# Layer 2 of a two-layer graph attention network on one core: who adds x, who sums the last rows of a tile, who makes the second norm's statistics

## The chip, the cores and the metric

The kernel runs on one core of one Trainium2 chip. The metric is the device time of one execution in microseconds (us). The kernel before the change has a median of 5286.99 us in three runs (5283.68 to 5294.54). Engines are called as the profile calls them: PE is TensorE (PEld its weight loads), DVE is VectorE, ACT is ScalarE, POOL is GpSimd, SP is SyncE.

## The reference, cut to what matters

Two layers of graph attention over 10000 nodes and 170000 edges (80000 in both directions and a loop for each node), with a layer norm and a residual behind each, and one more layer norm at the end. The change touches layer 2 (one head, 768 columns) and what follows it:

```python
def gat_conv(x, edge_index, W, a_src, a_dst, bias, heads, out_ch, concat):
    ...
    alpha = e / (s[dst] + 1e-16)                       # softmax over the edges of a node
    msg = xl[src] * alpha[:, :, None]
    out = jax.ops.segment_sum(msg, dst, num_segments=n)
    ...
h = gat_conv(h, edge_index, W2, a_src2, a_dst2, b2, 1, OUT_DIM, False)
h = layer_norm(h, g2, be2)
h = h + (h1 @ Wr2 + br2)
...
x = _layernorm(x + h)                                  # the second norm: no scale, no shift
```

## The kernel before, in words

**Layers and tiles.** Nodes are sorted by their number of edges and cut into 79 tiles of 128 nodes. Every node of a tile gets the same number n of edge places, so that a tile is n "rows": row k holds, on each of the 128 partitions, the 770 numbers (768 columns and two logits) of the k-th neighbour of that partition's node. There are 1371 rows in all, some 17 a tile. The order of tiles (`turns`) mixes long and short ones; in the middle of layer 2 tiles of 15 and 20 rows alternate. Layer 1 ends about 3200 us into the span, layer 2 fills the rest.

**The ring.** Rows of layer 2 lie in a ring of `RING2` = 41 places (`ring`). POOL fetches each by an indirect DMA (line 472), in order; a tile's first row, the node's own, comes by SP instead (line 501). `ring.fetch(FIRST[t] + k + 1 + ring.size)` stands behind row k in the loop, so a place is fetched anew when both engines that use its row are done with it.

**Two engines sum a tile.** DVE adds columns 0 to 511 of each row, times the row's weight, to an accumulator in SBUF (`acc`, in `weigh`, line 573): one SCALAR_TENSOR_TENSOR a row. PE adds columns 512 to 767 (`summed` in `weights_of`): for each row ACT multiplies the identity by the weights of the 128 nodes (line 1298, the "diagonal"), and PE multiplies the diagonal with the row's 256 columns (line 1299) into PSUM, into columns 768 to 1023 of the same PSUM tile `big` that holds the tile's residual. An f32 matmul is two matmuls in the profile. Diagonals lie in 5 buffers of 4 (`DIAGONALS`, `G`): a buffer is used anew when all 4 matmuls of its last use are done.

**The residual.** `residual(t)` makes h1 @ Wr2 on PE: for 512 and then for 256 columns, first x, by a matmul with the identity (line 1350), then the 8 pieces of h1 (line 1353). x and h1 of a tile come by SP (`fetch_x`, lines 1257 and 1258), two tiles ahead.

**The norms.** `norms(t, ...)` is a generator that runs in four pieces in the loop of the next tile: (1) ahead of row 0, DVE makes the statistics of the first norm (`deviation`: BN_STATS, line 584, of two pieces of `acc` and of PE's 256 columns in `big`; BN_AGGR, line 586), ACT makes the inverse deviation by Ln and Exp (lines 588, 589); (2) at row 3, DVE scales and shifts (lines 598, 600), adds the residual (line 1363) and makes the statistics of the second norm (lines 584, 586, on `w`), ACT its inverse deviation; (3) at row 6, DVE makes minus mean over deviation (line 1367) and ACT the output (line 1369); (4) at row 9, POOL scatters it to DRAM (line 1371).

**The order.** All engines run their instructions in the order in which the program writes them. In the loop of tile t it is: `residual(t + 1)` on PE; piece 1 of `norms(t - 1)`; then the rows, and between them the other pieces, the softmax weights of tile t + 1 (`weights_of`, at row `turn`, some 5 or 6, and 3 rows later, DVE and ACT) and, with those, the diagonals and PE's matmuls for tile t + 1. Three of the 79 tiles are so long that their softmax is made in two parts (`cuts_of` gives three cuts).

Of the kernel before, what the change touches and what calls it, by code (L numbers as in the profile page):

```python
# [28 lines left out]
F32 = mybir.dt.float32  # L29
# [6 lines left out]
P = 128  # L36
# [16 lines left out]
DIAGONALS = 5  # L53
ON_PE2 = 512
SHARE = 4
# [31 lines left out]
def gnn_kernel(ctx, tc, x, x_cols, src, dst, src_col, dst_col, W1, a_src1, a_dst1, b1, g1, be1, Wr1, br1,  # L87
# [757 lines left out]
    def begin_layer2(mem):  # L845


        rest = mem.shape[1]

        def at_end(n):  # L850
            nonlocal rest
            rest -= n
            return mem[:, rest:rest + n]

        firsts = [(at_end(C1), at_end(D0)) for _ in range(min(2, NT))]
        for t, (hT, xt) in enumerate(firsts):
            nc.sync.dma_start(hT, h1_d[turns[t]])
            nc.sync.dma_start(xt, x_d[turns[t]])
# [376 lines left out]
    def ordered_layer2(mem, begun):  # L1235
# [4 lines left out]
        with tc.tile_pool(name="b2", bufs=1) as pool, tc.tile_pool(name="small2", bufs=2) as small, \  # L1240
# [4 lines left out]
            parts = pieces(w2.rearrange("p k n -> p (k n)")[:, :6 * C1], C1)  # L1245
            held = mem.shape[1] // R2
# [4 lines left out]
            def fetch_x(t):  # L1251

                if t < 2:
                    hT, xt = firsts[t]
                else:
                    hT, xt = parts[t % 2], parts[2 + t % 2][:, :D0]
                    nc.sync.dma_start(hT, h1_d[turns[t]])
                    nc.sync.dma_start(xt, x_d[turns[t]])
                return hT.rearrange("p (k n) -> p k n", n=P), xt

            ins = {0: fetch_x(0)}
# [3 lines left out]
            ins[1] = fetch_x(1)  # L1265
# [20 lines left out]
            def weights_of(t):  # L1286
# [7 lines left out]
                def summed(e, lo, hi, more=None, m=0):  # L1294
                    for k in range(lo, hi):
                        if (k - lo) % G == 0:
                            diagonals = pool.tile([P, G, P], F32, name="diagonals", bufs=DIAGONALS)
                        nc.scalar.activation(diagonals[:, (k - lo) % G, :], ident, AF.Copy, scale=e[:, k - lo, :])  # L1298
                        nc.tensor.matmul(to, diagonals[:, (k - lo) % G, :], ring.slot(at + k)[:, ON_PE2:C2],  # L1299
                                         start=False, stop=(k == n - 1), skip_group_check=True)  # L1300
                        if k - lo < m:
                            nc.tensor.matmul(more, diagonals[:, (k - lo) % G, :], ring.slot(at + k)[:, :ON_PE2],
                                             start=False, stop=(k - lo == m - 1), skip_group_check=True)
# [15 lines left out]
                summed(e, 0, cuts[1])  # L1319
# [23 lines left out]
            def residual(t):  # L1343


                hT, xt = ins.pop(t)
                r = ps_big.tile([P, 2 * BANK], F32, name="big")
                for c in range(0, C2, BANK):
                    d = min(C2, c + BANK)
                    nc.tensor.matmul(r[:, c:d], ident, xt[:, c:d], start=True, stop=False,  # L1350
                                     skip_group_check=True)
                    for j in range(K1):
                        nc.tensor.matmul(r[:, c:d], hT[:, j, :], wr2[:, j, c:d], start=False,  # L1353
                                         stop=(j == K1 - 1 and d < C2),
                                         skip_group_check=True)
                return r

            def norms(t, h, r, means):
# [8 lines left out]
                nc.vector.scalar_tensor_tensor(less, mean, -1.0, inv, op0=OP.mult, op1=OP.mult)  # L1367
                o = pool.tile([P, C2], F32, name="out")
                nc.scalar.activation(o, h, AF.Identity, bias=less, scale=inv)
# [14 lines left out]
            for t in range(NT):  # L1384
# [19 lines left out]
                for k in range(n):  # L1404
# [11 lines left out]
                    else:  # L1416
# [15 lines left out]
                if t + 2 < NT and t + 2 not in ins:  # L1432
                    ins[t + 2] = fetch_x(t + 2)
# [273 lines left out]
```

## Time and profile before

| | |
|---|---|
| time, median of 3 runs | 5286.99 us (5283.68 to 5294.54) |
| the profiled execution | 5287.85 us, span 5286.1 us, mean granted PE clock 0.943 |
| busy over the span: PE, DVE, ACT, POOL | 4742.8 (90%), 4326.7 (82%), 3084.4 (58%), 3432.3 (65%) us |
| moved over the span | HBM read 1426.26 MB, written 177.29 MB, 303 GB/s |

The profile is of one execution. Each row of a group says: line, engine, operation, output from inputs by the program's names, shapes, count; then busy us and mean ns of one; then the idle time of the engine just ahead of these instructions, and what ended most of it ("issue": nothing that the profile shows; "remote": a semaphore from elsewhere). `w` in a name is the SBUF memory of the layer's weights W2, which layer 2 uses again for h1, x and the normed tile. A row of the timeline says: start, duration, engine, line, operation, names, shape, count, and the idle time ahead of it.

### The profile page before, as it was taken

What the parts mean: (1) busy time and instruction counts of PE and PEld (TensorE: products, weight loads), DVE (VectorE), ACT (ScalarE), POOL (GpSimd) and SP (SyncE); (2) the same over time, 40 slices, a digit from 0 to 9 for tenths busy, and PEclk for the clock granted to TensorE, in tenths of its full rate; (3) what the DMA queues carried; (4) which work ended last, traced back from release to release, by engine and by line L of the source; (5) the groups of instructions that cost most, each with busy time, mean ns of one, the idle gap of its engine ahead of it and who ended that gap; (6) DMA issues with size and microseconds to landing.
All of it is one profiled execution on the core that took longest, in us unless ns stands there. A gap on an engine that the chain in (4) does not pass through costs nothing. (4 is left out here: it accounts for less than half of the span.)

```text
span 5286.1 us, 57927 instructions
## 1 busy us (share of the span) xinstructions
PE 4742.8 (90%) x14012; PEld 2650.4 (50%) x14012; DVE 4326.7 (82%) x7168; ACT 3084.4 (58%) x8710; POOL 3432.3 (65%) x3722
## 2 busy tenths in 40 slices
PE   9999998999999979899999997888888887888886
PEld 4444444554444434444445554555555555555554
DVE  7887877998998988889999975877878777777776
ACT  5744446899999988898999862322222322222222
POOL 6867756666777766677766626666666666666664
PEclk9999998999999989999999998889898898888888
DMA  4423459999999989999999959988899898888885
GB/s 153 131 94 129 112 174 338 350 365 367 382 387 395 376 299 339 344 372 380 376 373 370 349 199 328 327 316 313 313 320 315 310 320 305 305 299 301 303 302 191
DMA packets 433439, 1588.37 MB, mean 300 GB/s; under 512 B 77207, under 2 KB 82135, under 8 KB 433094
## 3 DMA queue, kind: packets, MB, share of 16 engines
q0 software_dynamic: 321040, 1283.72, 67.4%
q1 hardware_dynamic: 99490, 269.38, 14.1%
q10 hardware_dynamic: 12564, 31.47, 1.8%
q8 instruction: 118, 1.93, 0.1%
q14 instruction: 227, 1.86, 0.1%
HBM read 1426.26 MB, written 177.29 MB: 303 GB/s over the span
## 5 line engine op out<-in xcount | busy, mean ns | idle before, releaser
L472 POOL DMA_INDIRECT ring<-table,slots x2663 | 2636.4, 990 | 1490.6 <-issue 569.8
L562 ACT ACTIVATE ring<-ring,e 128x256 f32<-128x256 f32 x4468 | 1823.6, 502 | 65.7 <-DVE e L981 34.3
L573 DVE SCALAR_TENSOR_TENSOR acc<-ring,e,acc 128x512 f32<-128x512 f32 (+1 forms) x2280 | 1454.0, 638 | 104.2 <-PE acc L936 27.1
L569 DVE TENSOR_TENSOR acc<-acc,ring 128x1024 f32<-128x1024 f32 x869 | 1070.2, 1231 | 80.7 <-ACT ring L562 16.9
L1353 PE MATMUL big<-wr,w 128*128 128x512 f32 (+1 forms) x2464 | 877.3, 501 | 148.9 <-issue 147.4
L1299 PE MATMUL big<-ring,diagonals 128*128 128x256 f32 x2742 | 723.9, 419 | 182.6 <-issue 166.2
L1161 PE MATMUL half<-w,hT 128*128 128x512 f32 (+1 forms) x2528 | 844.0, 486 | 5.5 <-issue 5.2
L179 PE MATMUL big<-wr,xT 128*128 128x512 f32 x1896 | 836.4, 598 | 0.3 <-ACT xT L897 0.3
L1299 PEld LDWEIGHTS big<-ring,diagonals 128*128 128x128 f32 x2742 | 582.4, 213 | 323.4 <-issue 220.1
L1298 ACT ACTIVATE diagonals<-ident,e 128x128 f32<-128x128 f32 x1371 | 419.6, 388 | 546.9 <-PE big L1299 215.8
L1353 PEld LDWEIGHTS big<-wr,w 128*128 128x128 f32 x2464 | 480.6, 196 | 511.8 <-issue 482.7
L1161 PEld LDWEIGHTS half<-w,hT 128*128 128x128 f32 x2528 | 472.6, 189 | 349.7 <-issue 310.4
L179 PEld LDWEIGHTS big<-wr,xT 128*128 128x128 f32 x1896 | 358.0, 192 | 422.3 <-issue 421.6
L936 PE MATMUL acc<-ring,ident 128*128 128x512 f32 x992 | 469.5, 622 | 76.6 <-ACT ring L562 49.3
L588 ACT ACTIVATE sd<-mv,eps 128x1 f32<-128x1 f32 x237 | 69.3, 292 | 683.7 <-issue 261.1
L936 PEld LDWEIGHTS acc<-ring,ident 128*128 128x128 f32 x992 | 191.3, 198 | 317.0 <-issue 193.2
L694 ACT ACTIVATE scr<-scr 128x256 f32<-128x256 f32 x624 | 250.5, 403 | 160.7 <-DVE scr L687 155.6
L634 PE MATMUL one<-wr,mixed 128*128 128x512 f32 x702 | 307.6, 592 | 0.0
L699 POOL TENSOR_TENSOR row<-row,none 128x1024 f32<-128x1024 f32 x69 | 168.1, 2437 | 117.2 <-DVE scr L687 45.8
L634 PE MATMUL one<-w,xT 128*128 128x512 f32 x492 | 228.6, 602 | 7.7 <-DMA w<-in_W_dram 5.4
L584 DVE BATCH_NORM_STATS2 st<-big 128x6 f32<-128x256 f32 x79 | 33.4, 423 | 242.3 <-remote 122.8
L634 PEld LDWEIGHTS one<-wr,mixed 128*128 128x128 f32 x702 | 133.4, 190 | 167.9 <-issue 167.2
(239 smaller groups left out, 4334.0 us busy)
## 6 DMA issues: line engine op xcount, KB each, us to landing
ring<-table,slots POOLq DMA_INDIRECT x2663
h_d<-hT SPq DMA_DIRECT2D x79, 512.0 KB
table<-row SPq DMA_DIRECT2D x78, 516.0 KB
w<-h_d SPq DMA_DIRECT2D x77, 512.0 KB
table<-row SPq DMA_DIRECT2D x79, 385.0 KB
ring<-table SPq DMA_DIRECT2D x79, 385.0 KB
x_d<-xt SPq DMA_DIRECT2D x77, 384.0 KB
w<-x_d SPq DMA_DIRECT2D x77, 384.0 KB
```

The source lines that it names most:

```text
L179: nc.tensor.matmul(p[:, c:e], aT[:, j, :], w[:, j, c:e], start=(j == 0), stop=(j == k - 1))
L472: nc.gpsimd.indirect_dma_start(out=to, out_offset=None, in_=table, in_offset=bass.IndirectOffsetOnAxis(ap=index, axis=0), **more)
L562: nc.scalar.activation(row[:, s], row[:, s], AF.Copy, scale=e[:, h:h + 1])
L569: nc.vector.tensor_add(acc[:, :c], acc[:, :c], row[:, :c])
L573: nc.vector.scalar_tensor_tensor(acc[:, s], row[:, s], e[:, h:h + 1], (acc if first is None else first)[:, s], op0=OP.mult, op1=OP.add)
L634: nc.tensor.matmul(p, aT[:, j, :], w[:, j, :], start=(start and j == 0), stop=(j == k - 1), skip_group_check=True)
L694: nc.scalar.activation(m[:, s], m[:, s], AF.Copy, accum_out=row[:, C1 + i * H1 + h:C1 + i * H1 + h + 1])
L936: nc.tensor.matmul(acc[:, c:c + BANK], ident, ring.slot(q + k)[:, c:c + BANK], start=(k == 0), stop=(k == m - 1))
L1161: nc.tensor.matmul(q, hT[:, j, :], w2[:, j, c:c + q.shape[1]], start=(j == 0), stop=(j == K1 - 1))
L1298: nc.scalar.activation(diagonals[:, (k - lo) % G, :], ident, AF.Copy, scale=e[:, k - lo, :])
L1299: nc.tensor.matmul(to, diagonals[:, (k - lo) % G, :], ring.slot(at + k)[:, ON_PE2:C2], start=False, stop=(k == n - 1), skip_group_check=True)
L1353: nc.tensor.matmul(r[:, c:d], hT[:, j, :], wr2[:, j, c:d], start=False, stop=(j == K1 - 1 and d < C2), skip_group_check=True)
```

## The change

- **Last rows.** In a tile with one softmax part, the last n // 6 rows (`ALL_BY_VECTOR` = 6) get no diagonal and no matmul. DVE sums their columns 512 to 767 too, by one more SCALAR_TENSOR_TENSOR a row that reads and writes PE's sums in PSUM. PE then has 1189 rows in place of 1371; the other 182 are DVE's.
- **x.** PE no longer adds x. DVE adds it to the normed tile, in piece 2 of `norms`. SP loads x one tile ahead in place of two, behind the load of h1, always at row n // 2.
- **Second norm.** DVE's BN_STATS and BN_AGGR of the second norm go, and line 1367. ACT sums the 768 columns (a Copy with an accumulator), makes minus the mean, sums the squares of the differences (Square with an accumulator), makes the inverse deviation (Ln, Exp), the product of the two, and the output, all at row 6.
- **Diagonals.** 28 single places, used in turn, in place of 5 buffers of 4: 20 in a tile of their own, 8 in the unused ends (256 columns) of four pieces of `w`.

```diff
-DIAGONALS = 5
+DIAGONALS = 20
+ALL_BY_VECTOR = 6
...
+            diagonals = pieces(pool.tile([P, DIAGONALS * P], F32, name="diagonals"), P)
+            for part in parts[2:]:
+                diagonals += pieces(part[:, C1 - 2 * P:], P)
+            turning = itertools.cycle(diagonals)
...
+            def by_vector(t):
+                return SLOTS[t] // ALL_BY_VECTOR if len(cuts_of(t)) == 2 else 0
...
                 def summed(e, lo, hi, more=None, m=0):
                     for k in range(lo, hi):
-                        if (k - lo) % G == 0:
-                            diagonals = pool.tile([P, G, P], F32, name="diagonals", bufs=DIAGONALS)
-                        nc.scalar.activation(diagonals[:, (k - lo) % G, :], ident, AF.Copy, scale=e[:, k - lo, :])
-                        nc.tensor.matmul(to, diagonals[:, (k - lo) % G, :], ring.slot(at + k)[:, ON_PE2:C2],
-                                         start=False, stop=(k == n - 1), skip_group_check=True)
+                        diagonal = next(turning)
+                        nc.scalar.activation(diagonal, ident, AF.Copy, scale=e[:, k - lo, :])
+                        nc.tensor.matmul(to, diagonal, ring.slot(at + k)[:, ON_PE2:C2],
+                                         start=False, stop=(k == n - 1 - by_vector(t)), skip_group_check=True)
...
-                summed(e, 0, cuts[1])
+                summed(e, 0, cuts[1] - by_vector(t))
...
             def residual(t):
-                hT, xt = ins.pop(t)
+                hT = ins.pop(t)
...
-                    nc.tensor.matmul(r[:, c:d], ident, xt[:, c:d], start=True, stop=False,
-                                     skip_group_check=True)
                     for j in range(K1):
-                        nc.tensor.matmul(r[:, c:d], hT[:, j, :], wr2[:, j, c:d], start=False,
+                        nc.tensor.matmul(r[:, c:d], hT[:, j, :], wr2[:, j, c:d], start=(j == 0),
...
                 nc.vector.tensor_add(h, h, r[:, :C2])
-                mean, inv = deviation(small, pieces(h, C2 // 2))
+                nc.vector.tensor_add(h, h, xs.pop(t))
                 yield
-                less = small.tile([P, 1], F32, name="less")
-                nc.vector.scalar_tensor_tensor(less, mean, -1.0, inv, op0=OP.mult, op1=OP.mult)
                 o = pool.tile([P, C2], F32, name="out")
+                less, inv = (small.tile([P, 1], F32, name=n) for n in ("less", "inv"))
+                nc.scalar.activation(o, h, AF.Copy, accum_out=less)
+                nc.scalar.activation(less, less, AF.Copy, scale=-1.0 / C2)
+                nc.scalar.activation(o, h, AF.Square, bias=less, accum_out=inv)
+                nc.scalar.activation(inv, inv, AF.Ln, scale=1.0 / C2, bias=eps)
+                nc.scalar.activation(inv, inv, AF.Exp, scale=-0.5)
+                nc.scalar.activation(less, less, AF.Copy, scale=inv)
                 nc.scalar.activation(o, h, AF.Identity, bias=less, scale=inv)
...
                             weigh(acc, row, weights[:, k - lo], ON_PE2, None if k else b2_b)
+                            if k >= n - by_vector(t):
+                                sums = rs[t][:, C2:2 * C2 - ON_PE2]
+                                nc.vector.scalar_tensor_tensor(sums, row[:, ON_PE2:C2], weights[:, k - lo], sums,
+                                                               op0=OP.mult, op1=OP.add)
                     ring.fetch(FIRST[t] + k + 1 + ring.size)
-                    if t + 2 < NT and k == n // 2:
-                        ins[t + 2] = fetch_x(t + 2)
+                    if k == n // 2:
+                        if t + 2 < NT:
+                            ins[t + 2] = fetch_h(t + 2)
+                        if t + 1 < NT:
+                            xs[t + 1] = fetch_x(t + 1)
```

**How the order moves, at three places.** The names carry the numbers of their buffers: `big` is the PSUM tile, `w2` the memory of W2 with h1, x and the normed tile in it, `wr1` the memory that holds Wr2. In brackets stand the semaphores waited for: DMASW is the landing of a gather, DMAHW that of a load by SP. On PE, from the last row of a tile of 20 rows to the addition of b2 in the next, before:

```order
L1299 MATMUL big_27355<-ring_4269,diagonals_27482 128x256 [waits DMASW0_49,Activation_49]
L1350 MATMUL big_27498<-w2_88,ident_70 128x512 [waits DMAHW4_49,DVE_49,PE_49]
L1353 MATMUL big_27498<-wr1_89,w2_88 128x512 [waits DMAHW3_49]
L1353 MATMUL big_27498<-wr1_89,w2_88 128x512 x7
L1350 MATMUL big_27498<-w2_88,ident_70 128x256
L1353 MATMUL big_27498<-wr1_89,w2_88 128x256 x8
L1308 MATMUL big_27498<-b2_22697,ident_70 128x256
```

and of the change, after a tile of 20 rows too, of which PE has 17:

```order
L1311 MATMUL big_27285<-ring_4269,diagonals_22685 128x256 [waits DMASW0_49,Activation_49]
L1363 MATMUL big_27415<-wr1_89,w2_88 128x512 [waits DMAHW0_49,DVE_49,PE_49]
L1363 MATMUL big_27415<-wr1_89,w2_88 128x512 x7
L1363 MATMUL big_27415<-wr1_89,w2_88 128x256 x8
L1320 MATMUL big_27415<-b2_22696,ident_70 128x256
```

The two matmuls with the identity on x are gone, and nothing has come in their place; the wait for x's landing went with them. On DVE, from the last rows of a tile of 15 rows to the first row of the next, before:

```order
L573 SCALAR_TENSOR_TENSOR acc_28223<-ring_4269,e_28119,acc_28223 128x512 [waits DVE_49] x5
L584 BN_STATS st_28365<-acc_28223 128x6 [waits DVE_49]
L584 BN_STATS st_28365<-big_28064 128x6 [waits PE_49]
L586 BN_AGGR mv_28369<-st_28365 128x2 [waits DVE_49]
L573 SCALAR_TENSOR_TENSOR acc_28364<-ring_4269,e_28259,b2_22697 128x512
```

and of the change, in the same tile:

```order
L574 SCALAR_TENSOR_TENSOR acc_27826<-ring_4269,e_27723,acc_27826 128x512 [waits DVE_49] x4
L1439 SCALAR_TENSOR_TENSOR big_27677<-ring_4269,e_27723,big_27677 128x256 [waits PE_49]
L574 SCALAR_TENSOR_TENSOR acc_27826<-ring_4269,e_27723,acc_27826 128x512 [waits DVE_49]
L1439 SCALAR_TENSOR_TENSOR big_27677<-ring_4269,e_27723,big_27677 128x256 [waits DVE_49]
L585 BN_STATS st_27956<-acc_27826 128x6 [waits DVE_49]
L585 BN_STATS st_27956<-big_27677 128x6 [waits DVE_49]
L587 BN_AGGR mv_27960<-st_27956 128x2 [waits DVE_49]
L574 SCALAR_TENSOR_TENSOR acc_27955<-ring_4269,e_27855,b2_22696 128x512
```

DVE's wait for PE's last matmul of the tile (PE_49) has moved up from the statistics of PE's columns to the first of the last two rows, so that these rows stand behind it. On DVE, piece 2 of the norms (`norm0` and `norm1` are the scale and shift), before:

```order
L598 SCALAR_TENSOR_TENSOR w2_88<-acc_28223,mv_28369,norm0_90 128x512
L598 SCALAR_TENSOR_TENSOR w2_88<-big_28064,mv_28369,norm0_90 128x256
L600 SCALAR_TENSOR_TENSOR w2_88<-w2_88,sd_28371,norm1_91 128x768 [waits DVE_49,Activation_49]
L1363 TENSOR_TENSOR w2_88<-w2_88,big_28064 128x768 [waits DVE_49]
L584 BN_STATS st_28384<-w2_88 128x6 [waits DVE_49]
L586 BN_AGGR mv_28387<-st_28384 128x2 [waits DVE_49]
```

and of the change:

```order
L599 SCALAR_TENSOR_TENSOR w2_88<-acc_27826,mv_27960,norm0_90 128x512
L599 SCALAR_TENSOR_TENSOR w2_88<-big_27677,mv_27960,norm0_90 128x256
L601 SCALAR_TENSOR_TENSOR w2_88<-w2_88,sd_27962,norm1_91 128x768 [waits DVE_49,Activation_49]
L1373 TENSOR_TENSOR w2_88<-w2_88,big_27677 128x768 [waits DVE_49]
L1374 TENSOR_TENSOR w2_88<-w2_88 128x768 [waits DMAHW2_49,DVE_49]
```

The statistics of the second norm are gone from DVE, and the addition of x, which waits for x's landing, stands there.

More of the change, by code (lines that the diff above doesn't have):

```diff
@@ L853, in at_end @@
             return mem[:, rest:rest + n]
-        firsts = [(at_end(C1), at_end(D0)) for _ in range(min(2, NT))]
-        for t, (hT, xt) in enumerate(firsts):
+        firsts = [at_end(C1) for _ in range(min(2, NT))]
+        for t, hT in enumerate(firsts):
             nc.sync.dma_start(hT, h1_d[turns[t]])
-            nc.sync.dma_start(xt, x_d[turns[t]])
         wr2 = wr1.rearrange("p k n -> p (k n)")[:, :K1 * C2].rearrange("p (k n) -> p k n", n=C2)
@@ L1249, in ordered_layer2, with fetch_h @@
             ring = Ring(table2, RING2, dict(zip(FIRST, (TURNS[t] for t in turns))), views, at)
-            def fetch_x(t):
[L1253 to L1261, printed above, removed]
+            def fetch_h(t):
+                if t < 2:
+                    hT = firsts[t]
+                else:
+                    hT = parts[t % 2]
+                    nc.sync.dma_start(hT, h1_d[turns[t]])
+                return hT.rearrange("p (k n) -> p k n", n=P)
+            def fetch_x(t):
+                xt = parts[2 + t % 2][:, :D0]
+                nc.sync.dma_start(xt, x_d[turns[t]])
+                return xt
+            ins = {t: fetch_h(t) for t in range(2)}
             ring.fetch(SLOTS[0])
```

7 lines of the change are left out of this document (3 added, 4 removed).

## The prediction

> **What bounds the kernel now.** Only layer 2 changes, so I first cut it out. The page gives the span; the view of busy time by stretches puts layer 2 beside a stretch of layer 1.
>
> ```profile
> span 5286.1 us, 57927 instructions
> ```
>
> ```profile
> core 0: us, PE busy (x) PEld busy (x) DVE busy (x) ACT busy (x) POOL busy (x), PEclk, DMA share, GB/s
> 2400.00:2500.00 100.00, 94.86 (x277) 47.73 (x278) 90.28 (x127) 88.71 (x226) 68.43 (x81) 1.00 1.01 376
> 3200.00:5280.00 2080.00, 1718.66 (x5664) 1159.59 (x5664) 1576.47 (x3152) 589.02 (x1846) 1301.28 (x1348) 0.89 0.87 304
> ```
>
> Layer 2 takes 2080 us, 26.3 us for each of 79 tiles. In it PE is busy 83% and DVE 76%, and the DMA engines are at 0.87 where layer 1 drives them to 1.01: nothing is full. So I read next, in the groups of that stretch with shapes kept apart, what ends each engine's idle time. These rows also carry the prices.
>
> ```profile
> line engine op names shapes xcount | busy us, mean ns | idle before us <-releasers
> L472 POOL DMA_INDIRECT ring<-table,slots x1269 | 1220.0, 961 | 711.2 <-issue 256.3 <-PE big L1299 226.1 <-remote 70.8
> L573 DVE SCALAR_TENSOR_TENSOR acc<-ring,e,acc 128x512 f32<-128x512 f32 x1286 | 966.9, 752 | 41.7 <-remote 5.2 <-DVE acc L573 0.4
> L1299 PE MATMUL big<-ring,diagonals 128*128 128x256 f32 x2728 | 720.7, 420 | 182.6 <-issue 166.2 <-DMA ring<-table,slots 7.4 <-ACT out L1369 2.4
> L1298 ACT ACTIVATE diagonals<-ident,e 128x128 f32<-128x128 f32 x1364 | 417.4, 388 | 545.8 <-PE big L1299 215.8 <-remote 84.1 <-DVE e L553 78.3
> L1353 PE MATMUL big<-wr,w 128*128 128x256 f32 x1232 | 324.7, 401 | 137.9 <-issue 136.5
> L1350 PE MATMUL big<-w,ident 128*128 128x512 f32 x154 | 85.3, 636 | 1.9 <-issue 1.9
> L1371 POOL DMA_INDIRECT out_dram<-out,order x79 | 81.3, 1029 | 64.3 <-POOLq L1654 21.0 <-ACT out L1369 19.9 <-issue 18.9
> L584 DVE BATCH_NORM_STATS2 st<-w 128x6 f32<-128x384 f32 x158 | 80.6, 552 | 2.7
> L600 DVE SCALAR_TENSOR_TENSOR w<-w,sd,norm 128x768 f32<-128x768 f32 x79 | 80.5, 1020 | 130.6 <-ACT sd L589 85.1 <-ACT sd L588 27.2 <-ACT diagonals L1298 11.4
> L1369 ACT ACTIVATE out<-w,less,sd 128x768 f32<-128x768 f32 x79 | 80.5, 1019 | 58.4 <-DVE less L1367 31.5 <-DVE acc L573 16.2 <-issue 7.4
> L1363 DVE TENSOR_TENSOR w<-w,big 128x768 f32<-128x768 f32 x79 | 75.3, 953 | 2.7
> L588 ACT ACTIVATE sd<-mv,eps 128x1 f32<-128x1 f32 x158 | 46.2, 292 | 659.6 <-issue 256.9 <-DVE mv L586 244.1 <-DVE st L584 158.4
> L1350 PE MATMUL big<-w,ident 128*128 128x256 f32 x154 | 46.0, 379 | 0.2 <-issue 0.2
> L598 DVE SCALAR_TENSOR_TENSOR w<-big,mv,norm 128x256 f32<-128x256 f32 x79 | 37.6, 476 | 0.0
> L584 DVE BATCH_NORM_STATS2 st<-big 128x6 f32<-128x256 f32 x79 | 33.4, 423 | 242.3 <-remote 122.8 <-PE big L1353 59.5 <-issue 42.6
> L589 ACT ACTIVATE sd<-sd 128x1 f32<-128x1 f32 x158 | 32.1, 203 | 12.1 <-remote 5.9 <-ACT sd L588 1.3
> L586 DVE BATCH_NORM_AGGREGATE mv<-st 128x2 f32<-128x12 f32 x79 | 16.5, 209 | 2.7
> ```
>
> Everyone waits for PE, and PE for nobody. POOL waits for places that L1299 frees, 226.1 us; ACT for free diagonals, 215.8; DVE for PE's sums ahead of its statistics, 242.3, and at L600, 130.6, for the deviation that stands on ACT behind those diagonals. PE's idle time is "issue" almost alone (166.2 + 136.5 us in these rows). I then looked at one tile in the timelines of PE, DVE and POOL, with the stretches around it.
>
> ```profile
> 4165.96 8.89 PE L1299 MATMUL big<-ring,diagonals 128*128 128x256 f32 x40 [0.34 <-issue]
> 4174.69 1.02 PE L1350 MATMUL big<-w,ident 128*128 128x512 f32 x2
> 4175.54 7.03 PE L1353 MATMUL big<-wr,w 128*128 128x512 f32 x16
> 4182.41 0.59 PE L1350 MATMUL big<-w,ident 128*128 128x256 f32 x2
> 4182.84 2.32 PE L1353 MATMUL big<-wr,w 128*128 128x256 f32 x10
> 4186.74 0.59 PE L1353 MATMUL big<-wr,w 128*128 128x256 f32 x2 [1.58 <-issue]
> 4189.56 0.59 PE L1353 MATMUL big<-wr,w 128*128 128x256 f32 x1 [2.23 <-issue]
> ...
> 4195.54 1.06 PE L1308 MATMUL big<-b,ident 128*128 128x256 f32 x2
> ```
>
> ```profile
> 4186.76 0.43 DVE L584 BATCH_NORM_STATS2 st<-big 128x6 f32<-128x256 f32 x1 [9.01 <-remote]
> ...
> 4187.38 0.69 DVE L573 SCALAR_TENSOR_TENSOR acc<-ring,e,b 128x512 f32<-128x512 f32 x1
> ```
>
> ```profile
> 4190.79 0.95 POOL L472 DMA_INDIRECT ring<-table,slots  x1 [0.30 <-issue]
> 4197.72 0.94 POOL L472 DMA_INDIRECT ring<-table,slots  x1 [5.98 <-PE big L1299]
> ```
>
> ```profile
> 4176.00:4186.00 10.00, 9.16 (x28) 5.10 (x27) 1.68 (x4) 0.99 (x3) 7.56 (x9) 1.00 0.94 331
> 4186.00:4196.00 10.00, 3.19 (x8) 1.89 (x8) 8.86 (x15) 0.99 (x4) 4.52 (x5) 0.65 0.79 288
> 4196.00:4204.00 8.00, 8.00 (x31) 6.71 (x30) 7.51 (x20) 4.57 (x14) 4.75 (x6) 0.79 0.88 272
> ```
>
> PE sums 20 rows in 8.9 us, makes the next residual, then stutters through its end: matmuls that wait for nothing come 1.5 to 2.2 us apart while POOL's gathers run, until 4195.5. DVE gets PE's sums, done at 4174.85, only at 4186.76. POOL stands still from 4191.7 until PE has freed a place. So PE paces layer 2 by its own stream: busy time, stutter, and a clock that falls in the stutter (0.65). Next come POOL, at least 1269 x (0.961 + 0.30) + 79 x (1.029 + 0.30) = 1705 us, the 0.30 being the gap ahead of each gather, and DVE, 1576 us.
>
> **The change part by part.** Counts are the built program's.
>
> *PE, last rows.* 1371 rows become 1189, 182 fewer, two matmuls each. At the mean of 420 ns that is 364 x 0.420 = 153 us; at the rate of the tile above (8.89 / 40 = 0.222 us) 81 us. The mean holds the stutter and the low clock, so it is the upper end.
>
> *PE, x.* The L1350 rows go: 85.3 + 46.0 = 131 us busy. At full rate they cost, from start to next start, 0.85 + 0.43 = 1.28 us a tile, 101 us. Together PE's stream shortens by 182 us at full rate, 284 at the means. I take 182: nothing says that the stutter shrinks in step.
>
> *DVE, last rows.* 182 operations on 128x256 that read and write PSUM: none in the trace. Below, L584 on `big`, which only reads PSUM (423 ns, 77 us); above, L573 on twice the columns (752 ns, 137 us); I take L598, the same operation and width with PSUM as an input: 476 ns, 87 us. [...]
>
> *DVE, x and statistics.* x adds 79 x 953 ns (L1363, same shape; here both inputs lie in SBUF) = 75 us. L584 on `w` and its L586 go: 80.6 + 16.5 = 97 us, and L1367, one 128x1 operation, priced like L586's 209 ns at most: up to 16 us, I take 12. DVE's net is 87 + 75 - 97 - 12 = +53 us (43 to 103 by the bounds), 1576 to 1629.
>
> *ACT.* Out: 182 x 388 = 71 us, and Ln and Exp of the second norm, 79 x (292 + 203) = 39. In: two passes over 768 columns at L1369's 1019 ns, 161 us, and four 128x1 operations of 203 to 292 ns, some 79 us. Net +130, 589 to 719 of 2080. Hidden: ACT is idle two thirds of the time, and makes diagonals a tile ahead of PE. Were that cover gone, PE would wait up to the 4.0 us of the new chain a tile. The chain stands ahead of the next tile's diagonals and of the first norm's deviation on ACT, and POOL's scatter waits for its end, with the gathers behind it. But the output comes three rows ahead of the scatter and has not been what the scatter waits for (19.9 us, at the end of the span).
>
> *SP and POOL.* No transfer is added. x now waits for DVE's addition of the x that it replaces, and stands behind h1; behind it wait only own rows and h1 that are wanted a tile later. Nothing, unless x lands later than one tile on.
>
> *Diagonals.* 28 places freed singly cover a tile's 13 to 17 and what PE has not done of the last one; ACT's 215.8 us go for the most part, and with them DVE's 130.6 at L600. I count nothing: PE is late in these tiles, and DVE meets the same lateness at the new wait, at the first of the last rows.
>
> *On the path.* PE's 182 us count in full, since its stream sets the pace. DVE's 53 I charge in full too: after its wait for PE it has rows still to sum, and the start of the next tile, which frees POOL's next place, is behind them. 182 - 53 = 129. The profiled execution took 5287.85 us (1.75 more than its span, 0.86 above the median of the three runs): 5287.85 - 129 = 5158.9, and 5158 as a median.
>
> **The rivals.**
>
> *Slower: the moved wait.* Where DVE waits for PE at the end of a tile, it now has behind the wait 182 / 76 = 2.4 rows of 0.752 + 0.476 us and two BN_STATS on `acc`, 0.8 us more: 3.7 us until the next tile's row 0. POOL, stopped at that row's place, gets it that much later, and PE's stutter lasts until POOL has stopped. At 3.7 us a tile, PE's 182 us are used up at 49 tiles of the 76. If DVE waits in 60, that is 222 - 182 = 40 us slower, 5328; in all, 5387. For: in the tile above PE's signal came 12 us late (4174.85 to 4186.76). Against: there PE itself came to its next addition of b2 only at 4195.54, 8.8 us after the signal, so that 3.7 us more on DVE would not yet have held it; 242.3 us of waits over 79 tiles are 3.1 a tile, so that many tiles have none; and with fewer rows PE signals sooner.
>
> *No change: PE's time becomes stutter.* If the stutter ends only when the gathers pause, a PE that is done sooner stutters longer. For: POOL's last gather started at 4190.8 and PE was free at 4195.5. Against: POOL has to stop for this in each tile, and it stops only because PE has not freed a place. 5287.
>
> *Small gain: the clock.* The clock was 1.00 ahead of the stutter, 0.65 in it and 0.79 after it. If each tile keeps its idle time with less work between, the mean of layer 2 falls from 0.89. Half way to the 0.79, at 0.84, the 1718.66 - 284 = 1435 us that are left to PE become 1435 x 0.89 / 0.84 = 1520, 85 more; 129 - 85 = 44, so 5243. [...]
>
> *Large gain.* PE's stream shortens by its means, 284 us, and DVE's additions fall into its waits (242.3 + 130.6 us): 5004, still above POOL's 1705 us.
>
> *Not what it says.* Diagonals in the ends of `w` could have tied PE to h1 or x; but in the built program those matmuls wait for the row's landing and for ACT alone. Under 2%, within the slower case.
>
> **How the numbers follow.** Forecast 0.50, large gain 0.15, clock 0.10, no change 0.09, moved wait 0.16. Faster by over 0.2% (11 us, about what a measurement of this kernel can tell) are the first three: 0.75; within it 0.09; slower 0.16. The forecast's own range is 5060 to 5230: PE's 182 to 284 against DVE's 43 to 103. The whole range reaches from 5050, which leaves out the further half of the large gain, to 5290, which leaves out the moved wait: together about 2 in 10.
>
> **What would show it.** Right: PE busy near 1718 - 284 = 1435 us in a layer 2 of some 1950, DVE near 1629, POOL's waits for PE below 226, ACT's for diagonals near none, L600's wait gone. The PSUM operation near 476 ns. Wrong if PE's "issue" idle grows by what its busy time loses (no change), if the new line's first row waits over 3 us in most tiles and POOL waits for DVE (moved wait), or if the clock falls well below 0.89.

## The result, and the profile after

The change takes 5210.69 us, median of 5 runs (5203.16 to 5214.41); before took 5286.95, median of 5 (5272.1 to 5294.54). The ratio is 0.9859, 95% interval 0.9843 to 0.9875: 76 us faster where 129 were forecast. The profiled execution took 5214.41 us.

Layer 2 is cut out at two like events: from the first matmul of the third tile's residual to some 6 us ahead of the end. The view by stretches, before:

```profile
3208.70:5280.00 2071.30, 1712.61 (x5645) 1154.50 (x5643) 1568.19 (x3135) 585.49 (x1834) 1295.01 (x1342) 0.89 0.87 304
```

and the change, columns as before (PE, PEld, DVE, ACT, POOL busy, clock, DMA share, GB/s):

```profile
span 5212.5 us, 56646 instructions
...
3217.70:5206.40 1988.70, 1556.70 (x4977) 1032.37 (x4975) 1601.98 (x3079) 710.52 (x2128) 1339.61 (x1341) 0.85 0.90 317
```

The stretch is 82.6 us shorter (it begins 9 us later in this execution). PE's busy time fell by 155.9 us, but its idle time rose from 358.7 to 432.0, by 73.3, and the clock fell from 0.89 to 0.85. DVE rose by 34 and ACT by 125. The groups of layer 2 in the change tell where PE's time stayed:

```profile
L473 POOL DMA_INDIRECT ring<-table,slots x1275 | 1262.8, 990 | 587.0 <-issue 279.6 <-PE big L1311 116.8 <-remote 105.9
...
L1363 PE MATMUL big<-wr,w 128*128 128x512 f32 x1232 | 559.5, 605 | 16.0 <-issue 15.8
L1311 PE MATMUL big<-ring,diagonals 128*128 128x256 f32 x1694 | 523.1, 448 | 296.5 <-issue 264.1 <-DMA ring<-table,slots 7.3 <-ACT inv L1382 3.3
...
L1363 PE MATMUL big<-wr,w 128*128 128x256 f32 x1232 | 288.1, 384 | 30.2 <-issue 30.2
L1310 ACT ACTIVATE diagonals<-ident,e 128x128 f32<-128x128 f32 x847 | 257.2, 387 | 69.7 <-DVE total L552 20.3 <-PE big L1311 13.7 <-DVE e L554 10.1
L1311 PE MATMUL big<-ring,w 128*128 128x256 f32 x672 | 199.1, 436 | 65.9 <-issue 56.5 <-remote 3.7 <-DMA ring<-table,slots 2.4
...
L1439 DVE SCALAR_TENSOR_TENSOR big<-ring,e,big 128x256 f32<-128x256 f32 x182 | 88.2, 485 | 107.7 <-PE big L1311 49.9 <-remote 41.9 <-issue 14.7
...
L601 DVE SCALAR_TENSOR_TENSOR w<-w,sd,norm 128x768 f32<-128x768 f32 x79 | 80.6, 1020 | 21.9 <-ACT sd L590 7.0 <-remote 5.5 <-DVE w L599 1.1
L1374 DVE TENSOR_TENSOR w<-w 128x768 f32<-128x768 f32 x79 | 75.7, 958 | 3.8 <-DVE w L1373 1.1
```

Two rows of PE's sums (L1311, by the memory of the diagonal) stand for before's one. Together they are 2366 matmuls and 523.1 + 199.1 = 722.2 us; before, 2728 took 720.7. So 362 matmuls less are no us less: each holds 0.305 us in place of 0.264. The idle time ahead of them rose from 182.6 to 362.4. At the residual it fell from 148.9 (137.9, and 11.0 in the row below) to 46.2:

```profile
L1353 PE MATMUL big<-wr,w 128*128 128x512 f32 x1232 | 552.6, 601 | 11.0 <-issue 10.8
```

The stutter (matmuls that wait for nothing and still come apart) did not go; it moved from the residual's end to the sums. One tile of the change in PE's timeline, POOL's stop in it, and ACT's last diagonals for this tile:

```profile
4842.74 10.48 PE L1363 MATMUL big<-wr,w 128*128 128x512 f32 x32
...
4853.49 0.59 PE L1311 MATMUL big<-ring,diagonals 128*128 128x256 f32 x2
4853.93 2.10 PE L1311 MATMUL big<-ring,w 128*128 128x256 f32 x9
4856.70 0.38 PE L1311 MATMUL big<-ring,w 128*128 128x256 f32 x1 [0.67 <-issue]
4858.78 0.38 PE L1311 MATMUL big<-ring,w 128*128 128x256 f32 x1 [1.71 <-issue]
4860.88 0.38 PE L1311 MATMUL big<-ring,w 128*128 128x256 f32 x1 [1.72 <-issue]
4861.60 2.06 PE L1311 MATMUL big<-ring,w 128*128 128x256 f32 x4 [0.35 <-issue]
```

```profile
4858.49 0.95 POOL L473 DMA_INDIRECT ring<-table,slots  x1 [0.31 <-issue]
4862.15 0.95 POOL L473 DMA_INDIRECT ring<-table,slots  x1 [2.71 <-PE big L1311]
```

```profile
4839.84 1.84 ACT L1310 ACTIVATE diagonals<-ident,e 128x128 f32<-128x128 f32 x6
```

The residual now runs at full rate (10.48 us for 32 matmuls). The sums stutter from 4856.0 to 4861.6, in steps of 0.7 us and its multiples, until 2.2 us after POOL has stopped at 4859.4. They do not wait for diagonals, which were done at 4841.7, nor for rows, whose logits went into the weights in these diagonals. The same holds when each of ACT's 1189 diagonals is put beside its two matmuls: in all but one of the 235 "issue" gaps over 0.3 us in the change's sums the diagonal was done before the gap began. Over the tiles from 3300 us on, the stutter begins 18.1 us (median) after POOL has gone on from its last stop, and 7.0 us after its scatter. PE's idle time per tile, in the mean of 76 tiles of layer 2, was 4.45 us before and is 5.39 now.

POOL's side gives the same gain. Its gathers' busy and idle time in layer 2 were 1220.0 + 711.2 = 1931.2 us and are 1262.8 + 587.0 = 1849.8: 81 less. Idle time fell by 124, but the gathers themselves take 43 us more, 990 ns in place of 961 (six more of them lie in this stretch). DVE's and POOL's timelines show where:

```profile
4874.10 1.02 DVE L601 SCALAR_TENSOR_TENSOR w<-w,sd,norm 128x768 f32<-128x768 f32 x1
4875.15 0.95 DVE L1373 TENSOR_TENSOR w<-w,big 128x768 f32<-128x768 f32 x1
4876.14 0.96 DVE L1374 TENSOR_TENSOR w<-w 128x768 f32<-128x768 f32 x1
```

```profile
4876.35 1.58 POOL L473 DMA_INDIRECT ring<-table,slots  x1 [0.30 <-issue]
4878.23 0.95 POOL L473 DMA_INDIRECT ring<-table,slots  x1 [0.30 <-issue]
```

The gather that started while DVE added x (L1374, both inputs in SBUF) ended 0.83 us after DVE did and took 1.58 us. Of 86 gathers and scatters that meet L1374 in this trace, 70 are lengthened, by some 40 us in all. What decides is which of the two began first. Of the gathers that began while L1374 ran (more than 0.08 us after its start and 0.15 us before its end), 62 of 63 are longer than 1.0 us; of the 19 that were already running when it began, none is. At the scaling L601, which has both inputs (w and norm) in SBUF too, it is 15 of 17, and none of 39; at a tile's first sum (L574 on `ring` and `b`, both in SBUF) 15 of 21, which end 0.81 us after it, as the other six do, and none of 54. Beside operations that read PSUM none is long, of 509 gathers that began during the sums that add to `acc` (the kernel has `acc` in PSUM, not in SBUF), the scaling from PSUM or the addition of the residual. Before, 44 gathers of layer 2 were over 1.0 us, by 16 us in all; now 95 are, by 50.

### The profile page after: what moved, and what is told of

The parts are those of the page before. It is cut to its first block, busy times and chain, and to the rows that moved or that the text cites. A ratio compares the mean times of both kernels' runs of the same rounds, so it can differ in the third digit from the quotient of the medians.

```text
span 5212.5 us, 56646 instructions
## 1 busy us (share of the span) xinstructions
PE 4580.7 (88%) x13332; PEld 2524.8 (48%) x13332; DVE 4359.7 (84%) x7113; ACT 3210.2 (62%) x9002; POOL 3481.6 (67%) x3722
## 5 line engine op out<-in xcount | busy, mean ns | idle before, releaser
L473 POOL DMA_INDIRECT ring<-table,slots x2663 | 2677.3, 1005 | 1366.0 <-issue 588.7
L574 DVE SCALAR_TENSOR_TENSOR acc<-ring,e,acc 128x512 f32<-128x512 f32 (+1 forms) x2280 | 1456.9, 639 | 97.4 <-PE acc L936 21.2
L1363 PE MATMUL big<-wr,w 128*128 128x512 f32 (+1 forms) x2464 | 834.9, 495 | 46.2 <-issue 46.0
L1311 PE MATMUL big<-ring,diagonals 128*128 128x256 f32 x1706 | 527.7, 449 | 298.6 <-issue 264.1
L1311 PEld LDWEIGHTS big<-ring,diagonals 128*128 128x128 f32 x1706 | 383.9, 227 | 427.4 <-issue 338.3
L544 ACT ACTIVATE e<-e 128x19 f32<-128x19 f32 (+14 forms) x82 | 17.6, 215 | 641.6 <-issue 243.1
L1310 ACT ACTIVATE diagonals<-ident,e 128x128 f32<-128x128 f32 x853 | 259.1, 387 | 70.7 <-DVE total L552 20.3
L589 ACT ACTIVATE sd<-mv,eps 128x1 f32<-128x1 f32 x158 | 46.1, 292 | 400.1 <-issue 159.9
L1311 PE MATMUL big<-ring,w 128*128 128x256 f32 x672 | 199.1, 436 | 65.9 <-issue 56.5
```

The lines of the kernel that those rows point to most:

```text
L473: nc.gpsimd.indirect_dma_start(out=to, out_offset=None, in_=table, in_offset=bass.IndirectOffsetOnAxis(ap=index, axis=0), **more)
L574: nc.vector.scalar_tensor_tensor(acc[:, s], row[:, s], e[:, h:h + 1], (acc if first is None else first)[:, s], op0=OP.mult, op1=OP.add)
L1310: nc.scalar.activation(diagonal, ident, AF.Copy, scale=e[:, k - lo, :])
L1311: nc.tensor.matmul(to, diagonal, ring.slot(at + k)[:, ON_PE2:C2], start=False, stop=(k == n - 1 - by_vector(t)), skip_group_check=True)
```

## The experiments

The experiments ran on four chips. Kernels of one letter ran on one chip, with before beside them; the change had its own runs, above. The diffs are against the change, but for a2, which is against before.

| kernel | before, us | kernel, us | ratio (95%) |
|---|---|---|---|
| a1_x_only | 5275.11 | 5254.81 | 0.9964 (0.995 to 0.9979) |
| a2_diagonals_only | 5275.11 | 5278.95 | 1.0 (0.9979 to 1.0021) |
| a3_all_but_rows | 5275.11 | 5229.79 | 0.9916 (0.9887 to 0.9945) |
| a4_all_but_stats | 5275.11 | 5201.81 | 0.9862 (0.9833 to 0.989) |
| b_rows4 | 5336.07 | 5256.34 | 0.9843 (0.9819 to 0.9866) |
| b_out_by_sp | 5336.07 | 5146.91 | 0.9644 (0.9621 to 0.9668) |
| b_scatter_later | 5336.07 | 5262.38 | 0.9857 (0.9836 to 0.9877) |
| b_h1_early | 5336.07 | 5262.29 | 0.9848 (0.9828 to 0.9868) |
| c_pause | 4929.98 | 5139.49 | 1.0427 (1.041 to 1.0445) |
| c_half_residual | 4929.98 | 4958.47 | 1.0057 (1.0041 to 1.0074) |
| c_no_x_load | 4929.98 | 4960.66 | 1.0063 (1.0047 to 1.008) |
| d_x_by_stt | 5339.53 | 5256.37 | 0.9856 (0.9831 to 0.9881) |

### Which part of the change gives what

**x alone.** The residual without x's matmuls, DVE's addition of x, SP's loads in the new order; DVE's statistics, the old diagonals and PE's rows stay.

```diff
-ALL_BY_VECTOR = 6
+ALL_BY_VECTOR = 1000
-DIAGONALS = 20
+DIAGONALS = 5
...
+                mean, inv = deviation(small, pieces(h, C2 // 2))
                 yield
-                nc.scalar.activation(o, h, AF.Copy, accum_out=less)
...
```

> Before with x alone moved: DVE adds it, PE's identity matmuls on x are gone; statistics, diagonals and rows as before. Theory 1 (the prediction: PE's stream paces, DVE's additions count in full): PE gives 101 us, DVE takes 75: 26 faster, 5261. Theory 2 (PE paces, but of what its stream loses a share comes back as idle time, as the whole change gave 76 of PE's 182 us; DVE's work costs nothing): 0.42 x 101 = 42 faster, 5245. Theory 3 (the diagonals' release, not PE's work, made the gain): 5287.

Measured: 0.36% or 19 us, 11 to 26 by the interval. Theory 3 falls. Theory 1's 26 lies at the edge of the interval, theory 2's 42 outside it. Of PE's 101 us at full rate a fifth came through.

**The diagonals alone.** Before, with the 28 single places.

```diff
-                        if (k - lo) % G == 0:
-                            diagonals = pool.tile([P, G, P], F32, name="diagonals", bufs=DIAGONALS)
+                        diagonal = next(turning)
```

> Before with the 28 single diagonals alone. Theories 1 and 2: no gain, 5287, though ACT's waits for free diagonals (215.8 us) and DVE's at the scale (130.6) go. Theory 3: most of the 76 us, some 5220.

Measured: nothing. ACT's 215.8 us of waits for diagonals and DVE's 130.6 behind them were in the shadow of PE, as counted.

**All but the last rows.**

```diff
-ALL_BY_VECTOR = 6
+ALL_BY_VECTOR = 1000
```

> The change without its last rows: PE sums all 1371 rows, x is on DVE, the statistics on ACT, 28 diagonals. Theory 1: PE gives 101 us, DVE is 34 us lighter (75 - 109): 135 faster, 5152, which is faster than the whole change. Theory 2: 0.42 x 101 = 42 faster, 5245, slower than the whole change by 34.

Measured: 44 us faster than before, so the last rows bring some 30 more. Theory 1 had this kernel at 135 and faster than the whole change; it falls, theory 2 gave 42.

**All but ACT's statistics.** DVE makes the second norm's statistics again.

```diff
+                mean, inv = deviation(small, pieces(h, C2 // 2))
                 yield
-                nc.scalar.activation(o, h, AF.Copy, accum_out=less)
...
```

> The change with the second norm's statistics back on DVE. Theory 1: DVE takes 109 us more than in the whole change: 5211 + 109 = 5320, and at the least some 50 more. Theory 2: DVE has room, 5211 within 10. Theory 4 (ACT's longer chain at row 6 delays the next diagonals and eats gain): faster than 5211 by 10 to 40.

Measured: 0.9862, the whole change within the interval, with these rows of DVE in layer 2 (the first is the last rows' line):

```profile
L1435 DVE SCALAR_TENSOR_TENSOR big<-ring,e,big 128x256 f32<-128x256 f32 x182 | 88.2, 484 | 58.9 <-PE big L1311 24.4 <-issue 16.1 <-remote 14.0
L585 DVE BATCH_NORM_STATS2 st<-w 128x6 f32<-128x384 f32 x158 | 80.6, 552 | 2.7
```

DVE does 80.6 + 16.5 us of statistics more and is idle ahead of the last rows 58.9 us in place of 107.7. These statistics go into DVE's idle time and cost nothing here; nor does ACT's longer chain in the whole change. That a3 gained 25 us over a1, though statistics and diagonals gain nothing elsewhere, is not settled; the two intervals nearly meet (0.995 and 0.9945).

**More last rows.**

```diff
-ALL_BY_VECTOR = 6
+ALL_BY_VECTOR = 4
```

> The change with the last n // 4 rows on DVE in place of n // 6, some 120 rows more. Theory 1 (DVE counts in full): PE gives 120 x 2 x 0.222 = 53 us, DVE takes 120 x 0.485 = 58: 5211 to 5220. Theory 2 (DVE has room, 0.4 of PE's saving is kept): 20 faster, some 5190. If DVE's room is used up by now, 5230 or more.

Measured: 0.9843 against the change's 0.9859: 8 us faster, within the intervals, and between the two theories (0.9843 of 5287 is 5204), so that the time does not tell them apart. The trace shows where the work went. DVE's 109 rows more take 53 us, and its idle time ahead of them is 72.7 us in place of 107.7. PE's two rows of sums are busy 684 us in place of 722, but the idle time ahead of them is 432 in place of 362: what PE sheds comes back as idle time again.

### What starts and ends the stutter

**The output by SP.** The rows of the output stand in another order in DRAM.

```diff
-                nc.gpsimd.indirect_dma_start(
-                    out=out, out_offset=bass.IndirectOffsetOnAxis(ap=nodes(turns[t]), axis=0),
-                    in_=o, in_offset=None, bounds_check=N - 1, oob_is_err=False)
+                m = min(P, N - turns[t] * P)
+                nc.sync.dma_start(out[turns[t] * P:turns[t] * P + m, :], o[:m, :])
```

> The change with the output written by SP, tile after tile, in place of POOL's scatter to the nodes' rows (the output's rows stand in another order). PE's stutter begins 7.0 us after POOL issues the scatter and 18.1 us after POOL goes on from its last stop (medians), and both could be its start. Theory S (the scatter starts it): the stutter goes, PE's idle time per tile falls from 5.4 us to below 2, the time by 150 to 300 us. Theory P (POOL's run without a stop, and the DMA queues that keep up with it, start it): the idle time stays above 4 us, the time falls by at most POOL's 79 x 1.4 = 110 us.

**The scatter later.**

```diff
-                    if k in (LEAD, 2 * LEAD, 3 * LEAD):
+                    if k in (LEAD, 2 * LEAD, 4 * LEAD):
```

> The change with the scatter at row 12 in place of 9. Theory S: the stutter begins 7 us after the scatter as now, so some 3 to 4 us later after POOL's last stop (21 to 22 us). Theory P: it begins 18 us after POOL's stop, as now, 3 us after the scatter. Time within 30 us of 5211 by either.

Theory S falls by both. Without a scatter PE stutters all the same (idle 4.5 us a tile in the mean, where theory S had it below 2); its timeline, and POOL's two gathers that end a stop:

```profile
4900.54 2.32 PE L1311 MATMUL big<-ring,w 128*128 128x256 f32 x10
4902.70 0.38 PE L1311 MATMUL big<-ring,diagonals 128*128 128x256 f32 x1
4903.68 0.38 PE L1311 MATMUL big<-ring,diagonals 128*128 128x256 f32 x1 [0.60 <-issue]
4905.81 0.38 PE L1311 MATMUL big<-ring,diagonals 128*128 128x256 f32 x1 [1.75 <-ACT inv L1382]
4907.23 3.83 PE L1311 MATMUL big<-ring,diagonals 128*128 128x256 f32 x17 [1.05 <-issue]
```

```profile
4884.34 0.96 POOL L473 DMA_INDIRECT ring<-table,slots  x1 [2.82 <-DVE acc L574]
4907.79 0.96 POOL L473 DMA_INDIRECT ring<-table,slots  x1 [2.65 <-PE big L1311]
```

It begins at 4903.1, 18.7 us after POOL went on, and ends 2.1 us after POOL stopped at 4905.1. With the scatter at row 12, in PE's and POOL's timelines:

```profile
4918.82 2.97 PE L1311 MATMUL big<-ring,diagonals 128*128 128x256 f32 x13
4923.49 0.38 PE L1311 MATMUL big<-ring,diagonals 128*128 128x256 f32 x1 [1.70 <-issue]
```

```profile
4902.82 0.95 POOL L473 DMA_INDIRECT ring<-table,slots  x1 [2.68 <-remote]
4917.87 1.50 POOL L1386 DMA_INDIRECT out_dram<-out,order  x1 [0.30 <-issue]
```

It begins at 4921.8, 19.0 us after POOL went on and 3.9 after the scatter (medians of all tiles 18.0 and 4.1). The onset is tied to POOL's run. And the 79 scatters that SP took over, some 79 x (1.13 + 0.30) = 113 us of POOL, came off the time in full: 5262.4 (the two other kernels of this chip that keep the change's order of work) less 5146.9 are 115 us. A tile lasts as long as POOL's run and its one stop, and it lasts as long as PE's stream and its stutter; both are true at once if each ends the other, as the times above say.

**h1 early.**

```diff
-                    if k == n // 2:
-                        if t + 2 < NT:
-                            ins[t + 2] = fetch_h(t + 2)
...
+                    if k == LEAD + 1 and t + 2 < NT:
+                        ins[t + 2] = fetch_h(t + 2)
...
```

> The change with the load of h1 at row 4 in place of n // 2; x stays. In the change the DMA engines are at 1.0 while SP's loads and the gathers run together, and PE runs at its full rate; PE's stutter begins some 3 us after their share has fallen to 0.87. Theory B (it comes when only gathers are in the queues, and goes when others join): the 512 KB come in the stretch where it begins, and it begins 2 to 3 us later or is shorter; idle time per tile down from 5.4, time down by 20 to 100 us. Theories S and P: onset unchanged, 5211 within 15.

Inconclusive: no change in time or onset, but the load did not come earlier either. SP's waits from 4000 us on (us in total, times, longest) show why:

```profile
SPq L1262 <- remote: 479.5, 23, 23.8
SPq L1262 <- PE big L1311: 444.4, 22, 24.5
```

SP waits some 20 us for PE's signal that h1's place is free, and that comes when the stutter ends, as in the change.

**Three kernels on a chip without the stutter.** On the third chip before took 4930 us, 7 to 8% less than on the others. These three were meant to tell the stutter's theories apart, and could not.

```diff
+            rests = pool.tile([P, 256], F32, name="rests")
...
+                    if k == n - 4:
+                        for _ in range(6):
+                            nc.gpsimd.memset(rests, 0.0)
```

> The change, and ahead of the gather that follows row n - 4 POOL writes zeros to 256 columns that nobody reads, six times: some 2 us in each tile in which it issues no gather, about half way between its stops. Theory Q (PE stutters when POOL has gathered some 18 us without a rest, and any rest ends or prevents it): the stutter begins 18 us after the rest or not at all; PE's idle time falls from 5.4 us a tile to 3 or less, POOL's stops for PE shrink by about the 2 us that the rest takes; time 5211, within 50 us either way. Theory R (only PE's own lateness makes POOL stop, and the rest does nothing for PE): PE's idle time stays at 5 us or more and the rests come on top: 79 x 2 = 158 us slower, less what the stops absorb, 5270 or more.

```diff
-                    for j in range(K1):
+                    for j in range(K1 // 2):
...
```

> The change with 4 of the 8 pieces of h1 left out of the residual: PE's stream is 79 x 8 x 2 x (0.43 + 0.215) / 2 = 410 us shorter at full rate, all else as it is. Theory 1 (PE's stream alone paces): 410 faster, 4800, unless POOL's 1705 us stop it at 4920. Theory 2 (of what PE sheds 0.42 are kept): 172 faster, 5040. Theory F (POOL's issue time and one stop a tile, which stays because PE stutters until POOL stops, are a floor that is nearly reached): at most 60 faster, 5150 or more, and PE's idle time grows by 4 us a tile.

```diff
-                nc.sync.dma_start(xt, x_d[turns[t]])
+                if t < 2:
+                    nc.sync.dma_start(xt, x_d[turns[t]])
```

> The change with x loaded for the first two tiles alone, so that DVE adds old values afterwards: 384 KB of some 8 MB a tile leave the DMA queues. If DMA throughput (share 0.90) sets the pace, 0.047 x 1989 = 90 us faster; if PE's stutter begins when SP's loads have been worked off, it begins some 5 us sooner after POOL's stop and PE's idle time grows; if neither, 5211 within 15 and the onset at 18 us.

For c_no_x_load, PE's timeline in one tile, two groups of layer 2, and PE's waits (us in total, times, longest):

```profile
4625.96 5.81 PE L1312 MATMUL big<-ring,w 128*128 128x256 f32 x16
4631.61 2.75 PE L1312 MATMUL big<-ring,diagonals 128*128 128x256 f32 x12
4634.20 10.48 PE L1364 MATMUL big<-wr,w 128*128 128x512 f32 x32
4644.52 0.59 PE L1321 MATMUL big<-b,ident 128*128 128x256 f32 x2
```

```profile
L473 POOL DMA_INDIRECT ring<-table,slots x1233 | 1231.0, 998 | 375.8 <-issue 103.0 <-PE big L1312 69.8 <-DMA ring<-table,slots 54.6
...
L1440 DVE SCALAR_TENSOR_TENSOR big<-ring,e,big 128x256 f32<-128x256 f32 x179 | 86.5, 483 | 0.0
```

```profile
PE big L1312 <- ACT diagonals L1311: 175.5, 36, 10.3
PE big L1312 <- ACT w L1311: 96.0, 15, 8.7
```

No step of 0.7 us is left. PE waits for diagonals, and DVE waits nowhere for PE (L1440, 0.0). POOL's 375.8 us of idle time are 1233 gaps of 0.30: it never stops. So POOL's issue alone paces layer 2 there. c_half_residual, with 410 us less for PE, has the same time (1.0057 and 1.0063) and the same gathers:

```profile
L473 POOL DMA_INDIRECT ring<-table,slots x1230 | 1226.9, 997 | 379.6 <-issue 107.9 <-PE big L1311 65.9 <-DVE acc L574 57.8
```

And c_pause is slower than these two by all of its rests: 180 us, against 79 x (2.17 + 0.42 - 0.30) = 181 by POOL's timeline:

```profile
4613.68 2.17 POOL L1445 MEMSET rests<- 128x256 f32 x6
4616.26 0.96 POOL L473 DMA_INDIRECT ring<-table,slots  x1 [0.42 <-issue]
```

Two kernels with the change in them, each relieved of something besides, are thus 28 to 31 us slower than before on this chip. The change itself was not run there. The lengthened gathers are the likely cost, since they add to POOL's time: 71 at the addition of x in c_no_x_load's trace, 45 us. Before has no such addition, but no trace shows before on that chip, so this stays argued.

**Another form for the addition of x.**

```diff
-                nc.vector.tensor_add(h, h, xs.pop(t))
+                nc.vector.scalar_tensor_tensor(h, h, 1.0, xs.pop(t), op0=OP.mult, op1=OP.add)
```

> The change with x added by SCALAR_TENSOR_TENSOR (times 1.0, plus x) in place of TENSOR_TENSOR: same numbers, same memory, 1.02 in place of 0.96 us on DVE. In the change 70 of the 86 gathers and scatters that meet TENSOR_TENSOR on x (both inputs in SBUF) end 0.82 us after it ends and take 0.6 us longer, 42 us in all. Theory L (that operation holds POOL's gather back, the other form doesn't, as the gathers that meet the scaling show, 18 long ones of 68): long gathers at this line go, POOL is some 42 us lighter; where POOL paces layer 2 without stops (before near 4930) the time is 40 below the 4958 that two kernels with the change in them gave there; where PE's stutter paces (before near 5280), 20 to 45 below 0.9859 of before. Theory M (any DVE operation on two SBUF inputs holds it): no change, or 5 us slower.

Theory L falls, M holds for this form. DVE's and POOL's timelines:

```profile
4759.14 0.96 DVE L1374 SCALAR_TENSOR_TENSOR w<-w 128x768 f32<-128x768 f32 x1
```

```profile
4759.47 1.47 POOL L473 DMA_INDIRECT ring<-table,slots  x1 [0.30 <-issue]
```

It takes the same 0.96 us, and 69 of 84 gathers and scatters that meet it are long, by some 42 us in all; the gather above ends 0.84 us after it. Of the gathers that began while it ran, all 69 are long; of the 13 that were already running, none is. Nor does the scaling L601 speak for theory L: 18 of the 19 gathers that began while it ran here are long. It looked harmless only because most gathers that meet it had begun earlier, or begin in its last 0.15 us.

## Why the prediction was right, and where it was not

The sign and the range held; the size was off, 129 us for 76. That it came as near as that is in part luck: PE's term was some 100 us too large, and DVE's 53, which cost nothing, took half of that back. Nor does the range of 5060 to 5230 come out of the terms named beside it, 182 to 284 less 43 to 103: these give 5047 to 5209, just short of the 5211 measured.

- *PE's 182 us on the path in full.* This step failed: "nothing says that the stutter shrinks in step" took the stutter as fixed, and it grew. PE's busy time fell by 156, which is 26 short of 182, and its idle time grew by 73: 83 were kept. The stutter begins some 18 us after POOL's last stop and ends some 2 us after its next (all tiles, and with the scatter moved or gone), so PE finishes its residual sooner and then stutters in its sums until POOL has run out of free places. The rival "PE's time becomes stutter" named that mechanism; it took all of PE's time for lost, and about half was.
- *The means as the upper end.* 364 matmuls at 420 ns were put at 153 us. Neighbouring matmuls overlap: 720.7 us over 2728 are 0.264 each, and the sums' busy time did not fall at all. The clock fell to 0.85, near the 0.84 of the clock's rival; since it falls where the stutter is (before, 0.65 from 4186 to 4196 us; in the change, 0.84 from 4860 to 4862 and 0.50 in the 2 us behind), no run here prices the two apart.
- *DVE's 53 us on the path.* Also wrong, the other way: 34 us more in the trace, and 97 us more on top of that were worth nothing in the time (a4_all_but_stats). DVE is still idle ahead of its last rows, 107.7 us at L1439, most often for PE.
- *The PSUM operation.* 485 ns measured for 476 taken. But the trace before did have operations that read and write PSUM: `acc` is a PSUM tile, so each L573 is one, on twice the columns. 256 columns fewer make L598 270 ns shorter (476 ns against the row below), and 752 - 270 = 482 would have been the price.

```profile
L598 DVE SCALAR_TENSOR_TENSOR w<-acc,mv,norm 128x512 f32<-128x512 f32 x79 | 58.9, 746 | 0.0
```

- *The diagonals at nothing, ACT's chain hidden.* Right (a2, a4). L600's wait went from 130.6 to 21.9 us.
- *The moved wait.* It did not come: POOL's waits for PE fell from 226.1 to 116.8 us and those for DVE's sums from 47.3 to 41.2, and DVE's idle time at the last rows is 1.4 us a tile in the mean, and over 3 us at 8 rows in all, where over 3 us in most tiles was the sign.
- *Not seen at all.* DVE's addition of x holds POOL's gathers, some 40 us in this trace. It was priced on DVE alone, though before's trace has such a hold: 21 of the 22 gathers that began while L600 ran were over 1.0 us. POOL was put third, at 1705 us and far from the end, though its run is one half of the cycle.

What makes PE stutter stays open. Its signals come late: half of those that the change's trace has from 3300 to 4800 us come 0.87 us or more after the end of the last instruction that gives one; DVE's and ACT's come within 0.012 us in the median, and on the chip without the stutter all 1411 of PE's come within 0.015 us. What holds them back, and why the stutter comes some 18 us into POOL's run and ends after its stop, no run here shows. The traces with a stutter also lack records: in this stretch before has 1084 of the 1386 signals that PE's instructions give, the change 1012 of 1272. But that does not account for PE's late signals, for the loss is not PE's alone. The change's trace has 658 of DVE's 2338 and 578 of ACT's 1485, and of PE's in layer 1, from 2000 to 3000 us, 457 of 661; on the chip without the stutter none are missing. So "remote" can be any signal without a record in these views, and whether the recording of events takes part in the stutter is open too.

## What to carry to other kernels

An engine that waits for nothing and still has gaps is not relieved by the sum of the work taken from it: first find what ends the gaps. Here POOL's stop did, and about half of the shed work (73 of 156 us) came back as gaps. Busy time per matmul is busy over count (here 0.264 us), not the mean length of one (0.420). Work added to an engine is also to be priced at what it holds up elsewhere: x's addition on DVE, of two SBUF operands, cost POOL 0.6 us for 62 of the 63 gathers that began beside it, while DVE had room for it.

## What the runs showed of the hardware

- One kernel took 5275, 5336 and 5340 us on three chips and 4930 on a fourth. Only the fourth showed no PE stutter, and there two kernels with the change in them were 0.6% slower than before. A gain of 1.4% belongs to the chips on which it was measured.
- In the change's trace a POOL gather that began while DVE ran an operation with two inputs in SBUF ended some 0.82 us after that operation: 62 of 63 at x's addition (L1374), 15 of 17 at the scaling with a factor from memory (L601), 21 of 21 at a tile's first sum (L574 with `b`), 15 of them over 1.0 us; 69 of 69 at the addition's other form (d_x_by_stt). A gather that had begun first was not delayed (0 of 19, 39 and 54; 0 of 13), nor was one that began beside a DVE operation that reads PSUM (0 of 509).
- Summing into PSUM on DVE (read and written) took 485 ns for 128x256 (L1439 of the change) and 752 for 128x512 (L573 of before); the scaling that only reads PSUM took 476 and 746 (L598 of before).
